# Attention weights transposed by transfers instead of on TensorE, in a two-layer graph kernel

## The chip, the cores and the metric

The kernel runs on one core of one Trainium2 chip. The core has five instruction queues that run on their own and meet at semaphores: TensorE (PE in the profile, its weight loads PEld), VectorE (DVE), ScalarE (ACT), GpSimd (POOL) and SyncE (SP), which here issues nearly all transfers. PE reads SBUF and writes PSUM, which the program uses as eight banks of 128 x 512 float32. The metric is device time in microseconds of one execution, the median of several.

## What is computed

There are 64 graphs of 256 nodes with 256 features, `x` (64, 256, 256), and an integer adjacency `adj` (64, 256, 256). Cut to what matters:

```python
# layer 0: three rounds of message passing with a GRU cell
A = (adj != 0)
h = x
for i in range(3):
    m = h @ weight[i]
    aggr = einsum('bst,bsd->btd', A, m)
    h = gru_cell(aggr, h, w_ih, w_hh, b_ih, b_hh)   # r, z: sigmoid; n: tanh; (1-z)*n + z*h
v = layernorm(x + h)
# layer 1: graph attention
Wh = v @ W
e = leaky_relu((Wh @ a1)[:, :, None] + (Wh @ a2)[:, None, :], 0.2)
attn = softmax(where(adj > 0, e, -9e15), axis=2)
out = layernorm(v + attn @ Wh)
```

All of it is float32. The gate matmuls are split into three parts (upper, lower, cross) whose sum comes close to float32.

## The kernel before

Graphs are worked on in **pairs**: 32 pairs p of two graphs (G = 2), each of C = 2 chunks of 128 nodes, so K = 4 chunks a pair. Each pair goes through three **blocks** (p, i), one for each round i of layer 0, and then through `attention`. Blocks are interleaved: one **turn** is the blocks (q, 0), (q-1, 1), (q-2, 2), and the attention of pair q-2 starts when its third block is done, beside the next turns.

**Order of the work.** Nothing is reordered after the program is written out; each engine takes its instructions in program order. The program makes this order with a small clock. `gates` writes the 72 matmuls of a block and calls `tick()` after every group of six (L469, L474): 12 ticks a block, 36 a turn. Everything else is a step put down for a tick with `at(t, step)` or `after(dt, step)` (L89, L93), and `tick` writes out all steps that are due; of steps of one tick, those put down first come first. So a tick fixes where an instruction stands in its queue and no time. After the last block the clock just jumps from step to step: this is the end of the run, with no gate matmuls beside it.

**A block's front.** `front` (L383), due from the start of the block ahead, prepares the operands: the hidden state's upper part on ACT (L419), its lower part on POOL (L423) and its cross part on DVE (L427), and the aggregation `aggregate` (L437) with its parts (L440 to L446). The tuples CLOSE, LOOSE and FIRST (L679 to L681) say at which ticks: the first six are turn, split, rest, aggregate, a_upper, a_rest, the last three h_upper, h_lower, h_cross.

**A block's gates.** `product` (L458) accumulates into two PSUM banks, pga and pgb; ACT empties the first (L471, L473) and DVE the second (L475). The gate chain behind goes through DVE, ACT (sigmoid and tanh, L484) and POOL (L492, L493, L498, L502), and ends with DVE's addition into the state hT (L505). `lags` are the ticks from the last product to tanh, blend and that addition.

**Transposes by transfer.** TensorE and a transfer can both transpose. The transfer takes 16-bit elements, so a float32 tile is seen as two 16-bit planes: a DMA transpose (`turn_half`, L295, or L345 for x) turns them, `gather` (L300, four transfers) brings the halves of each plane together, and two strided 16-bit copies, `put_together` (L278), interleave the planes to float32 again. Before the change x (from pair 5 on: `x_turned`, `x_joined`), the state between rounds (`h_turned`) and v (in `attention`) are turned so. In `put_together` ACT copies the upper plane; the lower goes to ACT for h (with `k`) and to DVE for x and v.

**Attention.** From tick t on (L544): the kept x is loaded again (L551) and h added to it (L553, vT), vT turned to v (L572 to L575), layer norm statistics (L578), `project` (L589), `spread` (L598, L600: ACT for k < 2, DVE for the others), `rows` (L608), `scores` (L612), the mask from the adjacency loaded a second time (L625), `masked` (L631), maximum (L633), exponentials `exps` (L636). Then `weights_T` transposes the weights on PE, four 128 x 128 pieces for each graph into a PSUM bank (L651), DVE copies the bank over the weights in SBUF (L669), `combine` multiplies by Wh (L659), `add` adds it to v (L665), and a second layer norm and the store follow (L676).

**Buffers** are tags of the pools, each with so many copies. Of `late`: "wh", "sc" and "vT" one, "v" two. Of `io`: "x" and "adj" one each. In "adj" stand, in turn, the adjacency, the second stage of x's and of h's (round 1) transposes, and the adjacency again. A tile waits until the last reader of its tag's former tenant is done. `room` gives the last two pairs' attention other buffers.

Of the kernel before, what the change touches and what calls it, by code (L numbers as in the profile page):

```python
# [9 lines left out]
F32 = mybir.dt.float32  # L10
# [9 lines left out]
P = 128  # L20
# [7 lines left out]
def kernel(  # L28
# [60 lines left out]
    def at(t, step):  # L89
        clock[1] += 1  # L90
        heappush(pending, (t, clock[1], step))
# [19 lines left out]
    def evacuate(dst, src):  # L111
        copies[0] += 1
        if copies[0] % 2:
            nc.scalar.copy(dst, src)
        else:
            nc.vector.tensor_copy(dst, src)

    def flat(t):
        return t.rearrange("p a b -> p (a b)")
# [155 lines left out]
            nc.tensor.transpose(pt[:, k * P:(k + 1) * P], src[:, k // C, k % C, d * P:(d + 1) * P], ident)  # L275
        after(1, lambda: evacuate(dst[:, d, :], pt))

    def put_together(dst, hi, lo, k=None):  # L278

        dst = dst.bitcast(U16).rearrange("p (n h) -> p h n", h=2)  # L280
        if k:
            dst = dst.rearrange("p h (k n) -> p h k n", k=k)
        nc.scalar.copy(dst[:, 1], hi)
        if k:
            nc.scalar.copy(dst[:, 0], lo)
        else:
            nc.vector.tensor_copy(dst[:, 0], lo)
# [17 lines left out]
    def h_turned(p, i, e):  # L305

        s = pairs[p]
        pool, tags, dt = ((late, ("wh", "sc"), (16, 19, 22)), (io, ("x", "adj"), (12, 22, 25)))[i]
        tmp = {}

        def first():
            tmp["a"] = first_of(pool.tile([P, G, C, D], F32, tag=tags[0], name=f"first_h{p}_{i}"))
            for d in range(C):
                turn_half(tmp["a"], s.hT, d)

        def second():
            tmp["b"] = second_of(pool.tile([P, G, C, D], F32, tag=tags[1], name=f"second_h{p}_{i}"))
            gather(tmp["b"], tmp["a"])

        def join(d):  # L320
            tmp[d] = work.tile([P, K, P], F32, tag="V", name=f"V{d}_{p}_{i}", bufs=1)
            put_together(tmp[d].rearrange("p k n -> p (k n)"),
                         *(tmp["b"][:, h, :, d * P:(d + 1) * P] for h in (1, 0)), k=K)

        def split(d):
            s.hi[d] = work.tile([P, K, P], F32R, tag=f"hi{d}", name=f"hi{d}_{p}_{i + 1}", bufs=1)
            nc.scalar.copy(s.hi[d], tmp[d])

        def rest(d):
# [28 lines left out]
    def x_joined(p):  # L358
        begin(p)
        s = pairs[p]  # L360
        for d in range(C):
            put_together(s.hT[:, d, :], s.halves[:, 1, d, :], s.halves[:, 0, d, :])

    def from_T(hT, d):
        pt = bank("pt")
# [178 lines left out]
    def attention(p, t):  # L544
# [47 lines left out]
        def spread(k):  # L592
            rs = s.rs[:, k:k + 1]
            for dst, src in ((s.s1[:, k:k + 1], pts[k][:, D:D + 1]),
                             (s.s2[:, k, :], pts[k][:, D + 1:D + 2].to_broadcast([P, P])),
                             (s.wh[:, k // C, k % C, :], pts[k][:, :D])):
                if k < 2:
                    nc.scalar.activation(dst, src, AF.Copy, scale=rs)  # L598
                else:
                    nc.vector.tensor_scalar(dst, src, rs, None, op0=ALU.mult)  # L600
        for k in range(K):
            at(t + 37 + k, lambda k=k: project(k))
            at(t + 38 + k, lambda k=k: spread(k))

        def rows():
            pts[0] = bank("s2")
# [16 lines left out]
        def mask():  # L623
            s.mask = work.tile([P, K, N], U8, tag="mask", name=f"mask_{p}", bufs=1)
            nc.vector.tensor_scalar(s.mask, loaded_adj.pop(p).rearrange("p g c n -> p (g c) n"), 0.0, None,  # L625
                                    op0=ALU.is_le)
        at(t + 38, adj_again)
        at(t + 43, mask)

        def masked():  # L630
            nc.vector.copy_predicated(flat(s.sc), flat(s.mask), neg.to_broadcast([P, K * N]))  # L631
# [4 lines left out]
            nc.scalar.activation(s.sc[:, k, :], s.sc[:, k, :], AF.Exp, bias=s.nm[:, k:k + 1],  # L636
                                 accum_out=s.sm[:, k:k + 1])
        for k in range(K):
            at(t + 47 + k // 2, lambda k=k: exps(k))

        def divide():

            nc.vector.tensor_mul(s.sm, s.sm, s.rs)
            nc.vector.reciprocal(s.sm, s.sm)
        at(t + 52, divide)

        def weights_T(g):
            pts[g] = bank("pt")
            for j in range(C):
                for c in range(C):  # L650
                    nc.tensor.transpose(pts[g][:, (j * C + c) * P:(j * C + c + 1) * P],  # L651
                                        s.sc[:, g * C + c, j * P:(j + 1) * P], ident)

        def combine(g):
            eT = s.sc[:, g * C:(g + 1) * C, :]
            pts[g] = bank("po")
            for c in range(C):
                for j in range(C):
                    nc.tensor.matmul(pts[g][:, c * D:(c + 1) * D], eT[:, j, c * P:(c + 1) * P], s.wh[:, g, j, :],  # L659
                                     start=(j == 0), stop=(j == C - 1))  # L660

        def add(g):
            for c in range(C):
                k = g * C + c
                nc.vector.scalar_tensor_tensor(s.v[:, g, c, :], pts[g][:, c * D:(c + 1) * D], s.sm[:, k:k + 1],  # L665
                                               s.v[:, g, c, :], op0=ALU.mult, op1=ALU.add)
        for g in range(G):
            at(t + 51 + g, lambda g=g: weights_T(g))
            at(t + 52 + g, lambda g=g: nc.vector.tensor_copy(flat(s.sc[:, g * C:(g + 1) * C, :]), pts[g]))  # L669
# [12 lines left out]


    blocks = []
# [43 lines left out]
    for n, (p, i) in enumerate(blocks):  # L728
        if n + 1 < len(blocks):
            np_, ni = blocks[n + 1]  # L730
            if ni == 0:
                if np_ < FROM:
                    after(1, lambda p=np_: begin(p))
                after(1, lambda p=np_: take_x(p))
                after(3, lambda p=np_: ones(p))
                nxt = np_ + 1
                if nxt < FROM:
                    after(7, lambda p=nxt: load_x(p))
                elif nxt < NP:
                    later = {}  # L740
                    after(25, lambda p=nxt, d=later: d.update(f=x_turned(p)))
                    after(29, lambda d=later: d["f"]())
                    after(32, lambda p=nxt: x_joined(p))
                    after(32, lambda p=nxt: load_x(p))
                after(5 if nxt < FROM else 34, lambda p=nxt: load_adj(p))
            front(np_, ni, clock[0], 
                  CLOSE if n and np_ == blocks[n - 1][0] or ni == 2 and np_ >= FROM else LOOSE if ni else FIRST)
        gates(p, i, (2, 3, 5) if n + 2 >= len(blocks) or blocks[n + 2][0] == p else (4, 5, 10))
        if i == L - 1:
            attention(p, clock[0])  # L750
        elif FROM <= p and p + i + 1 < NP:
            h_turned(p, i, clock[0])
# [32 lines left out]
```

## Time and profile before

| what | us |
|---|---|
| median of 3 runs | 2135.44 (2135.32 to 2135.72) |
| the profiled execution | 2135.01 |
| its span, first to last instruction | 2133.2 |
| PE busy in it | 2087.5 |
| DVE, ACT, POOL busy in it | 1788.7, 1609.8, 1605.2 |
| mean granted TensorE clock | 0.991 |

The span is 1.8 us shorter than the execution's own time; the rest lies around it. A row of a group reads: line, engine, operation, output<-inputs, shapes, count | busy time of all, mean ns of one | idle time of the engine just before them, and what ended it. Overlapping instructions count once in busy time. A row of a timeline is start, length, engine, line, operation, tiles and count; neighbours of one kind are merged.

### The profile page before, as it was taken

Reading aid. Unit: us, or ns where it says so; the run is one execution under the profiler, and the core shown is the slowest. Engines: PE = TensorE matmul, PEld = TensorE weight load, DVE = VectorE, ACT = ScalarE, POOL = GpSimd, SP = SyncE. Lnnn points to the kernel's source line nnn. Section 1 sums busy time; section 2 is a strip of 40 time slices with the busy share of each in tenths; the row PEclk is TensorE's granted clock in tenths of the full one; section 3 lists DMA queues with packets and bytes.
Section 4 is the critical chain, followed back from the end, with each engine's and each line's share of the span. In section 5 each row is a group of like instructions: output and inputs, shape, how many; then the busy total and the mean of one; then the engine's idle time right before and its main releaser. Section 6 shows DMA issues by size and latency. Waiting matters only on the chain.

```text
span 2133.2 us, 30903 instructions
## 1 busy us (share of the span) xinstructions
PE 2087.5 (98%) x10100; PEld 1748.8 (82%) x10100; DVE 1788.7 (84%) x2885; ACT 1609.8 (75%) x2938; POOL 1605.2 (75%) x1114
## 2 busy tenths in 40 slices
PE   8999999999999999999999999999999999999985
PEld 6788888888888888888888888888888888888864
DVE  5667788898889898888889888989888989888775
ACT  4566677778787777888777888787888787878664
POOL 6677687787788787788787787878777878778661
PEclk9999999999999999999999999999999999999997
DMA  4011324445545545445545544554544644543232
GB/s 128 30 40 40 67 73 119 99 99 129 115 103 129 120 107 129 109 100 128 129 109 119 110 111 116 129 120 108 129 102 110 135 119 99 131 111 85 50 75 74
DMA packets 416865, 220.68 MB, mean 103 GB/s; under 512 B 241792, under 2 KB 408448, under 8 KB 416704
## 3 DMA queue, kind: packets, MB, share of 16 engines
q1 hardware_dynamic: 414912, 216.86, 43.5%
q8 instruction: 80, 1.31, 0.3%
q10 hardware_dynamic: 1616, 1.57, 0.2%
q14 instruction: 81, 0.66, 0.1%
q0 software_dynamic: 176, 0.27, 0.1%
HBM read 69.74 MB, written 33.55 MB: 48 GB/s over the span
## 4 chain that ended last, share of the span: by engine, by line
PE 94%; DVE 2%; POOL 1%; ACT 1%; issue 1%; DMA 0%; POOLq 0%; ACTq 0%; SPq 0%; DVEq 0%
PE pga L466 48%; PE pgb L466 24%; PE pa L437 8%; PE po L659 5%; PE pwh L589 5%; PE pt L651 1%; PE s L608 1%; PE pt L367 1%; DMA rows_hH<-in_L_gnn_w_hh_dram 0%; PE pw L236 0%; POOL n L502 0%; DVE sc L631 0%; DVE cut L133 0%; POOL t L492 0%; DVE nm L633 0%
## 5 line engine op out<-in xcount | busy, mean ns | idle before, releaser
L492 POOL TENSOR_TENSOR t<-hT,n 128x512 f32<-128x512 f32 x192 | 253.1, 1318 | 391.1 <-ACT n L484 391.0
L466 PE MATMUL pga<-hH,whhH_whh 128*128 128x512 f32 x1152 | 378.2, 409 | 0.0
L466 PE MATMUL pgb<-hD,whhD_whh 128*128 128x512 f32 x1152 | 359.5, 393 | 1.2 <-DVE hD L136 1.2
L466 PE MATMUL pga<-hL,whhL_whh 128*128 128x512 f32 x1152 | 357.1, 391 | 0.0
L493 POOL TENSOR_TENSOR t<-t,z 128x512 f32<-128x512 f32 x192 | 291.3, 1517 | 15.1
L471 ACT ACTIVATE r<-pga 128x512 f32<-128x512 f32 x192 | 114.8, 598 | 242.4 <-PE pga L466 130.9
L502 POOL TENSOR_TENSOR n<-n,t 128x512 f32<-128x512 f32 x192 | 281.0, 1464 | 21.4 <-DVE t L475 11.1
L498 POOL TENSOR_TENSOR n<-n,r 128x512 f32<-128x512 f32 x192 | 288.4, 1502 | 4.5 <-DVE n L475 4.5
L475 DVE SCALAR_TENSOR_TENSOR r<-pgb,r 128x512 f32<-128x512 f32 x192 | 131.3, 684 | 166.4 <-ACT r L471 139.9
L133 POOL TENSOR_TENSOR hL<-hT,hH 128x1024 fp32r<-128x1024 f32 x96 | 255.7, 2664 | 13.3 <-ACT hH L130 13.2
L466 PEld LDWEIGHTS pgb<-hD,whhD_whh 128*128 128x128 f32 x1152 | 214.0, 188 | 55.2 <-issue 8.4
L466 PEld LDWEIGHTS pga<-hL,whhL_whh 128*128 128x128 f32 x1152 | 216.4, 188 | 47.9 <-POOL hL L133 0.4
L466 PEld LDWEIGHTS pga<-hH,whhH_whh 128*128 128x128 f32 x1152 | 206.3, 189 | 31.9
L437 PE MATMUL pa<-A,hi 128*128 128x256 f32 x768 | 200.0, 293 | 0.0
L437 PE MATMUL pa<-A,lo 128*128 128x256 f32 x768 | 192.0, 283 | 0.0
L136 DVE SCALAR_TENSOR_TENSOR hD<-hH,hT 128x1024 fp32r<-128x1024 f32 x96 | 186.4, 1942 | 0.0
L505 DVE TENSOR_TENSOR hT<-t,n 128x512 f32<-128x512 f32 x192 | 171.3, 893 | 5.6 <-POOL t L493 5.6
L484 ACT ACTIVATE r<-r,b_sum 128x512 f32<-128x512 f32 x192 | 140.4, 731 | 42.7 <-DVE r L475 42.0
L473 ACT ACTIVATE n<-pga,bh 128x512 f32<-128x512 f32 x192 | 133.5, 696 | 50.7 <-PE pga L466 46.4
L471 ACT ACTIVATE t<-pga 128x512 f32<-128x512 f32 x192 | 115.3, 601 | 57.3 <-DVE hT L505 38.2
L475 DVE SCALAR_TENSOR_TENSOR t<-pgb,t 128x512 f32<-128x512 f32 x192 | 131.0, 682 | 25.6 <-ACT t L471 22.5
L437 PEld LDWEIGHTS pa<-A,lo 128*128 128x128 f32 x768 | 146.3, 191 | 6.2 <-issue 0.2
(142 smaller groups left out, 5474.0 us busy)
## 6 DMA issues: line engine op xcount, KB each, us to landing
adj<-in_adj_dram SPq DMA_DIRECT2D x64, 512.0 KB, 4.2
second<-first SPq DMA_DIRECT2D x236, 128.0 KB, 3.2
second_h<-first_h SPq DMA_DIRECT2D x204, 128.0 KB, 3.4
x<-in_x_dram SPq DMA_DIRECT2D x32, 512.0 KB, 4.2
xT<-hT SPq DMA_DIRECT2D x32, 512.0 KB, 3.0
vT<-xT SPq DMA_DIRECT2D x32, 512.0 KB, 4.4
out_dram<-v SPq DMA_DIRECT2D x32, 512.0 KB, 3.2
first_h<-hT SPq DMA_TRANSPOSE x102, 3.5
```

The source lines that it names most:

```text
L133: eng.tensor_sub(dst, src, hi.bitcast(F32))
L136: nc.vector.scalar_tensor_tensor(dst, hi.bitcast(F32), 1.0 + U, src, op0=ALU.mult, op1=ALU.subtract)
L437: nc.tensor.matmul(pt[:, g * N:(g + 1) * N], h[:, g * C + c, :], s.A[:, g, c, :], start=(n == 0), stop=(n == len(todo) - 1))
L466: nc.tensor.matmul(pt, w[:, d, o * P:(o + 1) * P], m[:, d, :], start=n in (0, ends + 1), stop=n in (ends, len(todo) - 1))
L471: nc.scalar.activation(dst, a, AF.Copy, scale=1.0 + U)
L475: nc.vector.scalar_tensor_tensor(dst, b, -1.0 / U, dst, op0=ALU.mult, op1=ALU.add)
L484: nc.scalar.activation(dst, dst, func, bias=bias)
L492: nc.gpsimd.tensor_sub(t, h, n)
L493: nc.gpsimd.tensor_mul(t, t, z)
L498: after(2, lambda r=r, n=n: nc.gpsimd.tensor_mul(n, n, r))
L502: after(1, lambda n=n, t=t: nc.gpsimd.tensor_add(n, n, t))
L505: after(lags[2], lambda n=n, t=t, h=h: nc.vector.tensor_add(h, t, n))
```

## The change

- **Weights by transfer.** For pairs p < 30 (`by_dma = p < NP - 2`) `turn_weights` issues one DMA transpose for each graph from the weights `sc` into a new tile `eT`, which has the tag "v"; `gather_weights` brings the planes' halves back into `sc`'s place (four transfers each), and `join_weights` interleaves the planes into `eT` by two copies on ACT. `combine` reads `eT`, and `add` writes its result there instead of over v (`s.o`). Pairs 30 and 31 keep PE's transposes and DVE's copy.
- **Half-way results in v's place.** The transpose of vT goes into v's own tile instead of into "wh", and h's second stage of round 0 into "adj" instead of into "sc".
- **Copies of planes.** `put_together` is told the engines, upper plane first: h of round 0 ACT and DVE, h of round 1 DVE and ACT (both were ACT's); v ACT for both (the lower was DVE's); x as it was.
- **Timetable.** Ticks of most attention steps move, the lags of the gates become (2, 5, 9) for (4, 5, 10), and each round has its own tuple for the front.

The diff, cut to its core:

```diff
+    ENGINES = {"a": nc.scalar.copy, "v": nc.vector.tensor_copy, "g": nc.gpsimd.tensor_copy}
...
-    def put_together(dst, hi, lo, k=None):
...
 
...
-        nc.scalar.copy(dst[:, 1], hi)
-        if k:
-            nc.scalar.copy(dst[:, 0], lo)
-        else:
-            nc.vector.tensor_copy(dst[:, 0], lo)
+        for h, src in ((1, hi), (0, lo)):
+            ENGINES[engines[1 - h]](dst[:, h], src)
...
-        pool, tags, dt = ((late, ("wh", "sc"), (16, 19, 22)), (io, ("x", "adj"), (12, 22, 25)))[i]
+        pool, dt = ((late, (16, 19, 22)), (io, (12, 22, 25)))[i]
...
-            tmp["a"] = first_of(pool.tile([P, G, C, D], F32, tag=tags[0], name=f"first_h{p}_{i}"))
...
+            tmp["b"] = second_of(io.tile([P, G, C, D], F32, tag="adj", name=f"second_h{p}_{i}"))
             gather(tmp["b"], tmp["a"])
...
-                         *(tmp["b"][:, h, :, d * P:(d + 1) * P] for h in (1, 0)), k=K)
+                         *(tmp["b"][:, h, :, d * P:(d + 1) * P] for h in (1, 0)), "av" if i == 0 else "va", k=K)
...
-                at(e + dt[2] + 3 * d + n, lambda step=step, d=d: step(d))
+                at(e + dt[2] + (2, 4)[i] * d + n, lambda step=step, d=d: step(d))
...
-        at(t + 5, again)
-        at(t + 14, lambda: nc.vector.tensor_add(flat(s.vT), flat(s.vT), flat(s.hT)))
+        at(t + 7, again)
+        at(t + 13, lambda: nc.vector.tensor_add(flat(s.vT), flat(s.vT), flat(s.hT)))
...
 
             if d == 0:
-                s.first = first_of(room("wh", [P, G, C, D], p, "first"))
-            turn_half(s.first, s.vT, d)
+                s.v = room("v", [P, G, C, D], p)
+            turn_half(first_of(s.v), s.vT, d)
...
             s.halves = second_of(room("sc", [P, G, C, D], p, "second"))
-            gather(s.halves, s.first)
+            gather(s.halves, first_of(s.v))
...
         def join(g):
-            if g == 0:
-                s.v = room("v", [P, G, C, D], p)
...
-                         *(s.halves[:, h, ks].rearrange("p k d -> p (k d)") for h in (1, 0)))
+                         *(s.halves[:, h, ks].rearrange("p k d -> p (k d)") for h in (1, 0)), ("aa", "aa")[g])
         for d in range(C):
-            at(t + 20 + d, lambda d=d: turn(d))
-        at(t + 24, second)
+            at(t + 24 + d, lambda d=d: turn(d))
+        at(t + 29, second)
         for g in range(G):
-            at(t + 28 + g, lambda g=g: join(g))
+            at(t + 32 + g, lambda g=g: join(g))
...
-            s.rs, s.eps = layer_norm(s.v, f"a_{p}", (t + 31, t + 33))
-        at(t + 30, norm)
+            s.rs, s.eps = layer_norm(s.v, f"a_{p}", (t + 34, t + 36))
+        at(t + 34, norm)
...
-        at(t + 38, adj_again)
-        at(t + 43, mask)
+        at(t + 37, adj_again)
+        at(t + 41, mask)
...
-            at(t + 47 + k // 2, lambda k=k: exps(k))
+            at(t + 46 + k // 2, lambda k=k: exps(k))
...
-        at(t + 52, divide)
+        at(t + 51, divide)
...
+        def turn_weights(g):
+
+            if g == 0:
+                s.eT = late.tile([P, G, C, C, P], F32, tag="v", name=f"eT_{p}", bufs=2)
+            nc.sync.dma_start_transpose(s.eT[:, g].rearrange("p c j n -> p (c j n)").bitcast(U16)
+                                        .rearrange("p (q n) -> p q n", n=P),
+                                        s.sc[:, g * C:(g + 1) * C, :].rearrange("p c n -> p (c n)").bitcast(U16))
+
+        def planes(g):
+            return s.sc[:, g * C:(g + 1) * C, :].rearrange("p c n -> p (c n)").bitcast(U16).rearrange(
+                "p (h m n) -> p h m n", h=2, n=P)
+
+        def gather_weights(g):
+            gather(planes(g), s.eT[:, g].rearrange("p c j n -> p (c j n)").bitcast(U16).rearrange(
+                "p (m b n) -> p m b n", b=2, n=P))
+
+        def join_weights(g):
+            dst = s.eT[:, g].rearrange("p c j n -> p (c j n)").bitcast(U16).rearrange("p (n h) -> p h n", h=2)
+            for h in (1, 0):
+                ENGINES[("aa", "aa")[g][1 - h]](dst[:, h], planes(g)[:, h].rearrange("p m n -> p (m n)"))
+
         def combine(g):
-            eT = s.sc[:, g * C:(g + 1) * C, :]
             pts[g] = bank("po")
             for c in range(C):
                 for j in range(C):
-                    nc.tensor.matmul(pts[g][:, c * D:(c + 1) * D], eT[:, j, c * P:(c + 1) * P], s.wh[:, g, j, :],
+                    if by_dma:
+                        e = s.eT[:, g, c, j, :]
+                    else:
+                        e = s.sc[:, g * C + j, c * P:(c + 1) * P]
+                    nc.tensor.matmul(pts[g][:, c * D:(c + 1) * D], e, s.wh[:, g, j, :],
                                      start=(j == 0), stop=(j == C - 1))
...
         def add(g):
+
+            if by_dma:
+                s.o = s.eT.rearrange("p g c j n -> p g c (j n)")
+            else:
+                s.o = s.v
             for c in range(C):
                 k = g * C + c
-                nc.vector.scalar_tensor_tensor(s.v[:, g, c, :], pts[g][:, c * D:(c + 1) * D], s.sm[:, k:k + 1],
+                nc.vector.scalar_tensor_tensor(s.o[:, g, c, :], pts[g][:, c * D:(c + 1) * D], s.sm[:, k:k + 1],
                                                s.v[:, g, c, :], op0=ALU.mult, op1=ALU.add)
+        by_dma = p < NP - 2
         for g in range(G):
-            at(t + 51 + g, lambda g=g: weights_T(g))
-            at(t + 52 + g, lambda g=g: nc.vector.tensor_copy(flat(s.sc[:, g * C:(g + 1) * C, :]), pts[g]))
-            at(t + 54 + g, lambda g=g: combine(g))
-            at(t + 55 + g, lambda g=g: add(g))
+            if by_dma:
+                at(t + 50 + g, lambda g=g: turn_weights(g))
+                at(t + 52 + g, lambda g=g: gather_weights(g))
+                at(t + 56 + g, lambda g=g: join_weights(g))
+            else:
+                at(t + 51 + g, lambda g=g: weights_T(g))
+                at(t + 52 + g, lambda g=g: nc.vector.tensor_copy(flat(s.sc[:, g * C:(g + 1) * C, :]), pts[g]))
+            at(t + (58 if by_dma else 54) + g, lambda g=g: combine(g))
+            at(t + (58 if by_dma else 54) + 1 + g, lambda g=g: add(g))
...
-            nc.sync.dma_start(out[p * G:(p + 1) * G].rearrange("g (c p) d -> p g c d", p=P), s.v)
+            nc.sync.dma_start(out[p * G:(p + 1) * G].rearrange("g (c p) d -> p g c d", p=P), s.o)
...
-        at(t + 60, lambda: layer_norm(s.v, f"b_{p}", (t + 61, t + 64, t + 66, t + 70), s.eps, store))
+        at(t + 60, lambda: layer_norm(s.o, f"b_{p}", (t + 60 + 1, t + 64, t + 66, t + 71), s.eps, store))
...
     CLOSE = (5, 5, 5, 7, 8, 8), (6, 6, 7)
-    LOOSE = (2, 3, 4, 6, 7, 8), (5, 8, 10)
-    FIRST = (2, 1, 2, 6, 7, 8), (5, 8, 10)
+    EARLY = (2, 1, 2, 6, 7, 8), (5, 8, 10)
+    FIRST = (2, 1, 2, 7, 7, 8), (3, 10, 7)
+    SECOND = (2, 3, 4, 6, 7, 8), (3, 8, 10)
+    THIRD = (2, 3, 4, 7, 8, 9), (3, 6, 7)
...
-                after(3, lambda p=np_: ones(p))
+                after(2, lambda p=np_: ones(p))
...
-                    after(25, lambda p=nxt, d=later: d.update(f=x_turned(p)))
-                    after(29, lambda d=later: d["f"]())
-                    after(32, lambda p=nxt: x_joined(p))
-                    after(32, lambda p=nxt: load_x(p))
+                    after(26, lambda p=nxt, d=later: d.update(f=x_turned(p)))
+                    after(30, lambda d=later: d["f"]())
+                    after(33, lambda p=nxt: x_joined(p))
+                    after(33, lambda p=nxt: load_x(p))
                 after(5 if nxt < FROM else 34, lambda p=nxt: load_adj(p))
...
-                  CLOSE if n and np_ == blocks[n - 1][0] or ni == 2 and np_ >= FROM else LOOSE if ni else FIRST)
-        gates(p, i, (2, 3, 5) if n + 2 >= len(blocks) or blocks[n + 2][0] == p else (4, 5, 10))
+                  CLOSE if n and np_ == blocks[n - 1][0] else
+                  EARLY if np_ < FROM and not ni else (FIRST, SECOND, THIRD)[ni])
+        gates(p, i, (2, 3, 5) if n + 2 >= len(blocks) or blocks[n + 2][0] == p else (2, 5, 9))
```

More of the change, by code (lines that the diff above doesn't have):

```diff
@@ L276, in to_T, with put_together @@
         after(1, lambda: evacuate(dst[:, d, :], pt))
-    def put_together(dst, hi, lo, k=None):
+    def put_together(dst, hi, lo, engines, k=None):
         dst = dst.bitcast(U16).rearrange("p (n h) -> p h n", h=2)
@@ L307, in h_turned @@
         s = pairs[p]
-        pool, tags, dt = ((late, ("wh", "sc"), (16, 19, 22)), (io, ("x", "adj"), (12, 22, 25)))[i]
+        pool, dt = ((late, (16, 19, 22)), (io, (12, 22, 25)))[i]
         tmp = {}
         def first():
-            tmp["a"] = first_of(pool.tile([P, G, C, D], F32, tag=tags[0], name=f"first_h{p}_{i}"))
+            tmp["a"] = first_of(pool.tile([P, G, C, D], F32, tag=("wh", "x")[i], name=f"first_h{p}_{i}"))
             for d in range(C):
@@ L316, in second @@
         def second():
-            tmp["b"] = second_of(pool.tile([P, G, C, D], F32, tag=tags[1], name=f"second_h{p}_{i}"))
+            tmp["b"] = second_of(io.tile([P, G, C, D], F32, tag="adj", name=f"second_h{p}_{i}"))
             gather(tmp["b"], tmp["a"])
@@ L361, in x_joined @@
         for d in range(C):
-            put_together(s.hT[:, d, :], s.halves[:, 1, d, :], s.halves[:, 0, d, :])
+            put_together(s.hT[:, d, :], s.halves[:, 1, d, :], s.halves[:, 0, d, :], ("av", "av")[d])
     def from_T(hT, d):
@@ L596, in spread @@
                              (s.wh[:, k // C, k % C, :], pts[k][:, :D])):
-                if k < 2:
+                if k in (0, 1):
                     nc.scalar.activation(dst, src, AF.Copy, scale=rs)
@@ L602, in attention @@
             at(t + 37 + k, lambda k=k: project(k))
-            at(t + 38 + k, lambda k=k: spread(k))
+            at(t + 37 + 1 + k, lambda k=k: spread(k))
         def rows():
```

## The prediction

> **What bounds the kernel now.** I read the page first: busy shares, then the chain that ended last.
>
> ```profile
> span 2133.2 us, 30903 instructions
> PE 2087.5 (98%) x10100; PEld 1748.8 (82%) x10100; DVE 1788.7 (84%) x2885; ACT 1609.8 (75%) x2938; POOL 1605.2 (75%) x1114
> PE 94%; DVE 2%; POOL 1%; ACT 1%; issue 1%; DMA 0%; POOLq 0%; ACTq 0%; SPq 0%; DVEq 0%
> ```
>
> PE is on 94% of the chain. A busy PE may still be a slow one, so next come the totals of single stretches, one turn (63.46 us, below) in the middle and the end:
>
> ```profile
> 1000.00:1063.46 63.46, 63.46 (x310) 53.38 (x309) 55.89 (x90) 51.04 (x94) 49.91 (x35) 1.00 0.50 117
> 2067.00:2133.00 66.00, 34.88 (x134) 26.37 (x132) 41.29 (x104) 27.60 (x74) 12.40 (x16) 0.77 0.40 96
> ```
>
> Columns: length; busy of PE, PEld, DVE, ACT, POOL; granted clock; DMA share; GB/s. In mid-run PE has no gap at all: what it doesn't execute is saved, and a wait of another engine counts only once PE stands. The last gate matmul ends at 2067.4; the 66 us behind it are a chain of latencies through all engines, in which PE work is nearly free and latency is dear. So the change has two prices, one per stage.
>
> The length of a turn is read from the transpose of x, once a turn on SP's timeline (63.44 and 63.48 us apart):
>
> ```profile
> 1131.44 1.88 SPq L345 DMA_TRANSPOSE first<-in_x_dram  x1
> 1194.88 1.33 SPq L345 DMA_TRANSPOSE first<-in_x_dram  x1
> 1258.36 2.03 SPq L345 DMA_TRANSPOSE first<-in_x_dram  x1
> ```
>
> A turn has 36 ticks of 1.76 us.
>
> **PE's transposes.** The groups by shape, and PE's timeline where eight of them lie:
>
> ```profile
> L651 PE MATMUL pt<-ident,sc 128*128 128x128 f32 x256 | 41.9, 288 | 16.7 <-ACT sc L636 16.7
> ...
> L669 DVE COPY sc<-pt 128x512 f32<-128x512 f32 x64 | 42.9, 672 | 0.0
> ```
>
> ```profile
> 1010.86 0.63 PE L466 MATMUL pgb<-hD,whhD_whh 128*128 128x512 f32 x2
> 1011.32 0.60 PE L651 MATMUL pt<-ident,sc 128*128 128x128 f32 x4
> 1011.68 0.71 PE L466 MATMUL pga<-hH,whhH_whh 128*128 128x512 f32 x2
> 1012.23 0.62 PE L466 MATMUL pga<-hL,whhL_whh 128*128 128x512 f32 x2
> 1012.69 0.63 PE L466 MATMUL pga<-aH,wc1H_wc 128*128 128x512 f32 x2
> 1013.15 0.60 PE L651 MATMUL pt<-ident,sc 128*128 128x128 f32 x4
> 1013.51 0.72 PE L466 MATMUL pga<-aL,wc1L_wc 128*128 128x512 f32 x2
> 1014.06 0.62 PE L466 MATMUL pgb<-hD,whhD_whh 128*128 128x512 f32 x2
> ```
>
> Gate matmuls go at 0.456 us a pair (1012.23 to 1012.69). From 1010.86 to 1014.06 are five pairs, 2.28 us, but 3.20 passed: eight transposes cost 0.92 us, 0.115 each, for one attention. This isn't the 288 ns of a single one, which overlap. Here the Trainium skill would mislead: "TensorE: Matmul & The Clock Gate", Part 4, has about 275 ns for a PE transpose in a kernel. Durations here agree (288), yet 232 of them at 275 would be an estimated 64 us of saving; by start-to-start spacing it is 232 x 0.115 = 26.6. The spacing decides.
>
> Why 232: the 24 for pairs 29 to 31 all start after 2067.4 (at 2081.65, 2101.40, 2104.31, 2115.02), so pairs 0 to 28, 29 attentions, lie where PE is full. All 29 go to transfers: **-26.6 us**, a turn of 62.54. Pairs 30 and 31 keep PE; pair 29 is of the tail, below.
>
> **What takes their place,** per turn of 62.54 us, each beside PE's work:
>
> SP: two transposes and eight gathers. By tile, one first_h transpose takes SP 1.33 us (median), one second_h gather 0.62; landing 3.4 us for both. 2 x 1.33 + 8 x 0.62 = 7.6 us of issue on SP's 23.9 now (sum over the turn from 1194.88), so 31.5. They are due at ticks 14 to 17, behind the transpose of x and ahead of x's gather (18). That slot is idle now: SP's timeline has the transpose end at 1196.2 and the gather start at 1206.8, 10.6 us, plus one tick by which the gather's releaser moves back: 12.3. Needed: 3.4 (first landing) + 8 x 0.62 = 8.3. It fits with 4 us left; beyond that x's join, the next adjacency and the mask are late in turn.
>
> ACT: weights' planes, four copies at 0.77 us (L283), +3.1; v's low planes come from DVE, two, +1.5; four of the eight copies of h's planes leave, -3.1. Together +1.5 on 51.0: 52.6 of 62.54, 84%. The exponentials run ahead of the weights' joins by 10 ticks.
>
> DVE: L669 goes, -1.3; v's planes go, -1.4; four copies of h's planes come. Their price isn't in the trace, but the same copy is, twice:
>
> ```profile
> L287 DVE COPY v<-second x64: 444/468/1190, 205.0 to 2094.9; 128x512 uint16<-128x512 uint16 x64
> ...
> L287 DVE COPY hT<-second x54: 448/1554/1897, 258.8 to 1913.4; 128x512 uint16<-128x512 uint16 x54
> ```
>
> Bounds 0.45 and 1.9 us; the slow ones lie under POOL instructions in the timeline (at 1023.00 under hL's 3.4 us). The Trainium skill, "SBUF — State Buffer", says why and speaks against this change: VectorE and GpSimd share a port pair as an exclusive lock, the loser waits the other's whole instruction. With POOL busy 49.9 of 63.46 us, the rule would put nearly every copy at 1.9: 4 x 1.9 - 2.7 = +4.9, DVE at 60.8 of 62.54. By the means (692 and 1577 ns), between which I take the middle, 1.13: 4.5 - 2.7 = +1.8, 57.7 or 92%. I take the rows: some v copies met POOL and still cost 0.47. On the path: nothing, while DVE keeps up.
>
> The timetable: x, ones, mask and exponentials move by one tick, v's transfers by four or five, at no cost of work. The moved h_lower (10 for 8 in FIRST) keeps its place among POOL's instructions, between the additions of one gate and the next blend. Tanh two ticks earlier (lag 2 for 4) takes from POOL its largest wait, 391 us for ACT's n (12 a turn), but ACT now waits for POOL's addition: 0.6 to 1.4 us each where lag 2 already stands at the end (2045.51, 2072.15), six a turn, 4 to 8 us against ACT's 10 idle. Behind it on ACT stand evacuations of PSUM: PE has eight banks, and two fewer groups take them. From the end of each bank's last reader to the start of the eighth next group, the timeline leaves a median of 2.9 us for pga and 3.9 for pgb, so 1 to 2 us of lateness is absorbed. Likely cost 0; without that cover, up to a few us a turn. Single buffers get tighter: "adj" now holds h's first-layer planes too, five tenants a turn in a chain, and v's transpose (24) waits for the last addition of the pair before (24). Bounds: 0 (PE is full, so nothing here can gain) to +1.5 us a turn; I take 0.
>
> **The tail.** Here pair 29's weights go by transfer though PE is idle, and pair 30's and 31's work stands behind them in every queue. The chain now:
>
> ```profile
> 2081.00 1.83 ACT sc L636 x7
> ...
> 2084.12 3.02 PE po L659 x8
> ...
> 2093.15 0.48 ACT wh L598
> ...
> 2095.51 1.62 ACT sc L612 x4
> ...
> 2114.37 2.09 ACT sc L636 x8
> ```
>
> Exponentials of 29 end at 2083.0, pair 30's spread starts 2092.7, exponentials of 31 2114.4, the end 2133.2. The mask, now ahead of the last state addition, brings 29's exponentials to 2082.3 (two done at 2081.4). Then SP, in order: transpose 0 issued 2081.4, transpose 1 2083.0, gathers 0 from 2085.3 (landing), 2.5 us, gathers 1 from 2087.9, and only then pair 30's own gather, 2090.5 instead of 2077.2 (tick 53 for both, 29's pushed first); it lands about 2095.7. ACT copies in order: 29's planes 0, pair 30's 0 (2095.7), 29's 1, pair 30's 1, ends 2099.8. DVE statistics 2100.9, POOL's root 1.9 later: spread of 30 at 2102.8, **10 us late**. Pair 31's own transfers are behind too (landing 2103), but its joins now come after 30's scores, so 31's exponentials start near 2123: +8.7. Bounds: +2 (landings as short as the minimum, orders that loosen) to +14 (a slow landing more). I take **+8.7**.
>
> **Sum.** Profiled execution 2135.0 (span 2133.2): 2135.0 - 26.6 + 8.7 = 2117.1; the median of the runs is 0.4 above it, so **2117.5 us**.
>
> **Rivals.**
> 1. The tail hides it: pair 30's path finds slack, nothing lost, 2135.4 - 26.6 = 2109. For: POOL idles 15.5 us there. Against: SP's queue is strict. 0.12.
> 2. Part is given back: PE stands 0.3 us a turn over 29 turns for a bank or an operand (L484 behind POOL, or x late): 2117.5 + 8.7 = 2126. For: banks come free only some 3 us ahead. 0.20.
> 3. Slower: DVE becomes the bound, in the turns with h by transfer (26). Place: h's copies at ticks 13, 17, 34, 36, under POOL. At 1.58 each (the hT row's mean) DVE has 55.9 + 6.3 - 2.7 = 59.5 us of work, and its wait for ACT's r (139.9 us, 4.4 a turn) stays: 63.9, 1.4 over 62.54, x 26 = 36: 2154. It decides once turns grow by 17.9 / 29 = 0.62 us. Against: that wait shrinks when DVE is late. 0.13.
> 4. It doesn't do what it says: freed PE time is spent waiting for what a turn needs anyway, turn near 63.2, 2135. Against: no gap on PE in the mid-run stretch. 0.05.
>
> **Chances.** Main case 0.50, its own range 2112 to 2124 (tail +3 to +14). By a difference of 0.2% (4.3 us), about what can be told from no change: faster 0.82 (main, 1, 2), same 0.05, slower 0.13. Range: leaving out rival 3 and the far ends, 2105 to 2134.
>
> **What would show it.** Right: L651 with 16 instructions, L669 with 4; turns 62.5 us apart; PE still gapless to about 2008; in the tail, SP gathers of the weights ahead of pair 30's, and 29's weights to the end some 9 us longer, about 75 us from the last gate matmul. Wrong: gaps on PE before pga or pa with ACT or DVE named; turns over 63.1; h's copies on DVE at 1.6 us and more; x's gather late behind the weights' gathers.

## The result, and the profile after

The changed kernel takes **2111.6 us** (2109.8 to 2114.4) against 2135.4: a ratio of 0.989, interval 0.9873 to 0.9907. Forecast were 2117.5 us, range 2105 to 2134. The profiled execution took 2112.9 us, with a span of 2111.1, 22.1 less than before.

First the page: the span, busy times of the engines, and the engines' shares of the chain that ended last.

```profile
span 2111.1 us, 31355 instructions
PE 2053.3 (97%) x9860; PEld 1726.3 (82%) x9860; DVE 1769.4 (84%) x2863; ACT 1659.1 (79%) x3020; POOL 1611.8 (76%) x1114
PE 93%; DVE 2%; POOL 2%; DMA 1%; ACT 1%; SPq 1%; issue 0%; POOLq 0%; ACTq 0%; DVEq 0%
```

PE has 240 instructions fewer and still bounds the run; ACT has more to do, DVE hardly less, and SP's queue and the transfers hold 1% of the chain each, where the page before had 0%. The two stages, in the totals of stretches (length; busy of PE, PEld, DVE, ACT, POOL; clock; DMA share; GB/s):

```profile
1000.00:1062.50 62.50, 62.50 (x302) 52.82 (x302) 56.14 (x90) 52.28 (x96) 50.30 (x35) 1.00 0.62 134
2034.50:2111.10 76.60, 33.41 (x124) 25.02 (x123) 40.15 (x102) 34.91 (x87) 13.61 (x19) 0.72 0.37 89
```

PE is still full in mid-run. From the start of a (q, 0) block's first gate matmul to that of the next, a turn is now 62.37 us, 63.48 before. The last gate matmul starts at 2034.1, 32.9 us earlier than before (2067.0); what lies behind it has grown from 66.2 to 77.0 us. Both parts went the way that was forecast. The extra time at the end, on SP's and ACT's timeline (start, length, line, operation, tiles; idle time before and what ended it):

```profile
2049.98 2.61 SPq L655 DMA_TRANSPOSE eT<-sc  x2
2053.34 5.27 SPq L302 DMA_DIRECT2D sc<-eT  x8
2058.66 2.88 SPq L302 DMA_DIRECT2D second<-v  x4
2060.60 1.38 ACT L670 COPY eT<-sc 128x512 uint16<-128x512 uint16 x2 [9.67 <-DMA sc<-eT]
```

Pair 29's eight gathers (sc<-eT) come out ahead of pair 30's four (second<-v), and ACT stands 9.7 us for them. Pair 30's spread starts 36.9 us after the last gate matmul, 25.7 before.

Three copies of planes, in the groups by shape (count | busy, mean ns of one | idle before):

```profile
L286 DVE COPY V<-second_h 128x512 uint16<-128x512 uint16 x102 | 85.8, 841 | 0.9
L670 ACT COPY eT<-sc 128x512 uint16<-128x512 uint16 x120 | 84.3, 772 | 16.1 <-DMA sc<-eT 15.8
...
L286 DVE COPY hT<-second 128x512 uint16<-128x512 uint16 x54 | 33.3, 670 | 0.7 <-DMA second<-first 0.7
```

The four copies new on DVE take 0.84 us each, and those of x, one tick later than before, fell from 1.58 to 0.67: before, 24 of the 54 started under POOL's `hL` and took 1.9 us, now none does. So DVE stays at 56.1 us a turn.

### The profile page after: what moved, and what is told of

Read it like the earlier page. It is cut to its first block, busy times and chain, and to the rows that moved or that the text cites. A ratio compares the mean times of both kernels' runs of the same rounds, so it can differ in the third digit from the quotient of the medians.

```text
span 2111.1 us, 31355 instructions
## 1 busy us (share of the span) xinstructions
PE 2053.3 (97%) x9860; PEld 1726.3 (82%) x9860; DVE 1769.4 (84%) x2863; ACT 1659.1 (79%) x3020; POOL 1611.8 (76%) x1114
## 4 chain that ended last, share of the span: by engine, by line
PE 93%; DVE 2%; POOL 2%; DMA 1%; ACT 1%; SPq 1%; issue 0%; POOLq 0%; ACTq 0%; DVEq 0%
PE pga L465 48%; PE pgb L465 24%; PE pa L436 8%; PE po L680 5%; PE pwh L586 5%; PE s L605 1%; PE pt L366 1%; SPq L302 1%; DMA rows_hH<-in_L_gnn_w_hh_dram 0%; DMA v<-vT 0%; POOL t L491 0%; POOL n L501 0%; DMA second<-v 0%; POOL t L492 0%; PE pw L238 0%
## 5 line engine op out<-in xcount | busy, mean ns | idle before, releaser
L491 POOL TENSOR_TENSOR t<-hT,n 128x512 f32<-128x512 f32 x192 | 264.2, 1376 | 186.2 <-ACT n L483 186.0
L497 POOL TENSOR_TENSOR n<-n,r 128x512 f32<-128x512 f32 x192 | 316.1, 1646 | 73.6 <-ACT r L483 48.5
L465 PE MATMUL pga<-hH,whhH_whh 128*128 128x512 f32 x1152 | 370.6, 403 | 0.0
L492 POOL TENSOR_TENSOR t<-t,z 128x512 f32<-128x512 f32 x192 | 271.0, 1411 | 15.0
L135 POOL TENSOR_TENSOR hL<-hT,hH 128x1024 fp32r<-128x1024 f32 x96 | 258.3, 2691 | 10.6 <-ACT hH L132 10.5
L138 DVE SCALAR_TENSOR_TENSOR hD<-hH,hT 128x1024 fp32r<-128x1024 f32 x96 | 202.4, 2109 | 0.0
L483 ACT ACTIVATE n<-n,bi 128x512 f32<-128x512 f32 x192 | 138.9, 723 | 75.5 <-POOL n L501 75.4
L436 PE MATMUL pa<-A,hi 128*128 128x256 f32 x768 | 193.6, 285 | 0.2 <-DVE A L377 0.2
L504 DVE TENSOR_TENSOR hT<-t,n 128x512 f32<-128x512 f32 x192 | 187.6, 977 | 5.9 <-POOL t L492 5.9
L436 PE MATMUL pa<-A,lo 128*128 128x256 f32 x768 | 192.1, 283 | 0.0
L135 DVE TENSOR_TENSOR aL<-pa,aH 128x512 fp32r<-128x512 f32 x192 | 131.1, 683 | 63.8 <-ACT aH L132 63.7
L132 ACT ACTIVATE aH<-pa 128x512 fp32r<-128x512 f32 x192 | 115.9, 604 | 64.0 <-PE pa L436 64.0
L483 ACT ACTIVATE z<-z,b_sum 128x512 f32<-128x512 f32 x192 | 140.7, 733 | 18.9 <-DVE z L474 18.1
```

The lines of the kernel that those rows point to most:

```text
L135: eng.tensor_sub(dst, src, hi.bitcast(F32))
L138: nc.vector.scalar_tensor_tensor(dst, hi.bitcast(F32), 1.0 + U, src, op0=ALU.mult, op1=ALU.subtract)
L436: nc.tensor.matmul(pt[:, g * N:(g + 1) * N], h[:, g * C + c, :], s.A[:, g, c, :], start=(n == 0), stop=(n == len(todo) - 1))
L465: nc.tensor.matmul(pt, w[:, d, o * P:(o + 1) * P], m[:, d, :], start=n in (0, ends + 1), stop=n in (ends, len(todo) - 1))
L483: nc.scalar.activation(dst, dst, func, bias=bias)
L491: nc.gpsimd.tensor_sub(t, h, n)
```

## The experiments

Time is compared with runs of the kernel before on the same chip (2134 to 2135 us). "Turn" is the length of most turns from the eighth on (the first is the one with block (0, 0) alone), "end" the time from the last gate matmul's start to the end of the span. The time before the third turn varies from run to run (100.8 to 103.6 us). Where weights aren't turned at all, the attention output of pairs 0 to 29 is not the reference's.

### All weights on TensorE, in the new timetable

```diff
-        by_dma = p < NP - 2
+        by_dma = False
```

> The changed kernel with all pairs' weights on TensorE's transposes; timetable, lags and engines of the plane copies stay changed. Theory (the transposes are the gain): turns go from 62.37 to 63.3 us, 29 x 0.94 = 27 us are lost and the tail's 10.8 are won back: 2128, so 7 below the kernel before, from the timetable. Rival (the timetable is the gain): turns stay near 62.5, 2101 to 2105.

Measured 2129.1 us, ratio 0.9971 (0.9959 to 0.9982); turn 63.38, end 65.9: the theory. From the third turn to the last gate matmul it needs 1958.2 us, the changed kernel 1931.5, the kernel before 1963.8. So taking the 232 transposes off TensorE is worth **26.7 us** in this timetable, and the rest of the change, with the transposes left in, 5.6 us.

The 26.7 us don't come evenly. The first three turns with attention get 0.87 us each shorter, the later ones 1.0, and the last three together 0.33, though they hold two attentions. Two waits stand behind that. The first row is a wait of the kernel with all weights on TensorE, which the changed kernel doesn't have; the second, of the changed kernel, comes 1.3 us long in the last three turns, where TensorE stands for the state:

```profile
PEld po L680 <- ACT V L286: 6.0, 25, 0.2
PE pt L366 <- DVE hT L504: 1.3, 1, 1.3
```

### No turning of the weights, in the new timetable

```diff
             if by_dma:
-                at(t + 50 + g, lambda g=g: turn_weights(g))
-                at(t + 52 + g, lambda g=g: gather_weights(g))
-                at(t + 56 + g, lambda g=g: join_weights(g))
+                pass
```

with `combine` reading `sc` and the tile `eT` made in `add`.

> The changed kernel without any turning of the weights of pairs 0 to 29: no transfers, no joins, no transposes; the products take the weights as they are, so the attention output of these pairs is not the reference's. It shows what the transfers and joins cost where TensorE is full. Theory: nothing there, turns stay 62.37 us; only the tail is shorter by 10 to 14: 2098 to 2102. Rival (transfers cost TensorE hidden waits): turns shorter than 62.3, under 2095.

Measured 2102.0 us, turn 62.37, end 62.3: the theory. Transfers and joins cost TensorE nothing in mid-run; at the end they cost 14.7 us. Two turns of 63.85 stand out here, of which more below.

### No turning of the weights, in the old timetable

```diff
-            at(t + 51 + g, lambda g=g: weights_T(g))
-            at(t + 52 + g, lambda g=g: nc.vector.tensor_copy(flat(s.sc[:, g * C:(g + 1) * C, :]), pts[g]))
+            if p >= NP - 2:
+                at(t + 51 + g, lambda g=g: weights_T(g))
+                at(t + 52 + g, lambda g=g: nc.vector.tensor_copy(flat(s.sc[:, g * C:(g + 1) * C, :]), pts[g]))
```

> The kernel before without the transposes and the copy of the weights of pairs 0 to 29, which are used as they are, so that the attention output of these pairs is not the reference's. It prices the eight transposes in the old timetable. Theory: 29 x 0.92 to 0.94 = 27 us where TensorE is full and about 2 us in the tail: 2106. Rival (freed time is spent waiting in the old timetable for the cross part or a bank): turns over 62.9, 2115 or more.

Measured 2115.4 us, ratio 0.9907 (0.9892 to 0.9922): the theory's 2106 fell. Turns begin with 62.49 and settle at 62.87. The waits of PE's weight loads (who waits on whom: us in total, times, longest):

```profile
PEld s L608 <- DVE sc L600: 8.7, 25, 0.7
PEld pgb L466 <- issue: 8.4, 28, 0.3
```

The second row is in the profile of before too. The first had 0.3 us in all there: now TensorE's weight load reaches `rows` some 0.35 us a turn before DVE has spread the last chunk. From the third turn to the last gate matmul only 19.2 of the 26.7 us arrive. The same transposes are worth over a quarter less in the old timetable, because DVE's spread is not as early as TensorE has become: that wait, 8.7 us in all on the weight loads, is about what is missing.

### One tick of the old timetable

The wait marked "issue" lies at 1008.93 in the kernel before, just after the state's cross part hD ends on DVE (1006.51 + 2.31):

```profile
1006.51 2.31 DVE L136 SCALAR_TENSOR_TENSOR hD<-hH,hT 128x1024 fp32r<-128x1024 f32 x1
1008.93 0.30 PEld L466 LDWEIGHTS pgb<-hD,whhD_whh 128*128 128x128 f32 x2 [0.29 <-issue]
```

```diff
-    LOOSE = (2, 3, 4, 6, 7, 8), (5, 8, 10)
+    LOOSE = (2, 3, 4, 6, 7, 8), (5, 8, 8)
```

> The kernel before with one number changed: LOOSE has the state's cross part on VectorE at tick 8 instead of 10. Theory (28 waits of 0.29 us of the weight load of pgb<-hD, marked issue, are for this cross part and cost TensorE 0.13 us a turn): turns fall from 63.48 to 63.35 us, some 3.5 us in all: 2131. Rival (those waits are only the sequencer's): turns stay 63.48.

Measured **2175.5 us**, ratio 1.0192: neither theory nor rival. That wait is gone, and the first turns with attention (the fifth to the seventh) are 0.14 to 0.18 us shorter than in the kernel before. But from the ninth on turns are 65.19, with a new row:

```profile
PEld po L659 <- issue: 39.7, 25, 1.6
```

The timeline of DVE, ACT and, in the last row, PE shows what happened:

```profile
1012.77 3.36 DVE L136 SCALAR_TENSOR_TENSOR hD<-hH,hT 128x1024 fp32r<-128x1024 f32 x1
1016.05 0.68 DVE L475 SCALAR_TENSOR_TENSOR r<-pgb,r 128x512 f32<-128x512 f32 x1
1016.77 0.72 ACT L484 ACTIVATE r<-r,b_sum 128x512 f32<-128x512 f32 x1 [2.17 <-DVE r L475]
1017.40 0.71 ACT L484 ACTIVATE n<-n,bi 128x512 f32<-128x512 f32 x1
...
1018.60 1.28 ACT L636 ACT_TABLE_LOAD   x1
...
1029.20 1.97 PE L659 MATMUL po<-wh,sc 128*128 128x256 f32 x8 [1.22 <-DVE sc L669]
```

The cross part now runs ahead of the gate's r on DVE and takes 3.4 us there, beside `hL` on POOL (2.4 us from 1012.65); ACT waits 2.2 us for r, and the exponentials behind it come late. The transposed weights' copy on DVE is late in turn, and `combine` stands for it. Some 0.15 us a turn were won and 1.9 lost.

### Two ticks of the old timetable, without the turning

```diff
-    LOOSE = (2, 3, 4, 6, 7, 8), (5, 8, 10)
+    LOOSE = (2, 3, 4, 6, 7, 8), (5, 8, 8)
-        gates(p, i, (2, 3, 5) if n + 2 >= len(blocks) or blocks[n + 2][0] == p else (4, 5, 10))
+        gates(p, i, (2, 3, 5) if n + 2 >= len(blocks) or blocks[n + 2][0] == p else (4, 5, 9))
```

> The kernel before without any turning of the weights of pairs 0 to 29 (attention output of these pairs not the reference's), plus two numbers of the timetable: cross part of LOOSE at tick 8 instead of 10, the state's addition at lag 9 instead of 10. Without the two numbers turns were 62.87. Theory (there TensorE waits 0.35 us a turn for the last spread on VectorE, behind a state addition, and 0.13 for the cross part; these two numbers lift both): turns 62.37 to 62.45, about 2104. Rival (the wait comes from VectorE's load in that stretch, whatever the order): turns stay over 62.7.

Measured 2192.7 us, turns of 66.0: the theory fell. The kernel leaves the transposes out, so TensorE stands at other places than above:

```profile
PEld pgb L466 <- issue: 48.7, 23, 2.3
PEld pa L437 <- ACT n L484: 31.1, 23, 1.5
```

Which of the two numbers does this, and by what order, was not tried apart.

### The old lags

```diff
-        gates(p, i, (2, 3, 5) if n + 2 >= len(blocks) or blocks[n + 2][0] == p else (2, 5, 9))
+        gates(p, i, (2, 3, 5) if n + 2 >= len(blocks) or blocks[n + 2][0] == p else (4, 5, 10))
```

> The changed kernel with the gates' lags of the kernel before, (4, 5, 10) instead of (2, 5, 9). Theory (the earlier tanh and state addition take 0.1 to 0.4 us of waits a turn off TensorE once its transposes are gone): turns 62.5 to 62.8, 2115 to 2124. Rival (the lags matter to POOL's waits alone): turns stay 62.37, 2112.

Measured 2125.0 us, ratio 0.9953 (0.9933 to 0.9972), turn 62.64: the theory, with the time 1 us above its range. The lags are worth 13 us here by the medians, 12 from the third turn to the last gate matmul. The wait is DVE's addition of the gate sum:

```profile
PEld pga L465 <- DVE t L474: 10.5, 23, 1.0
```

### h's planes all on DVE, or all on ACT

```diff
-                         *(...), "av" if i == 0 else "va", k=K)
+                         *(...), "vv", k=K)
```

> The changed kernel with all eight copies of h's planes of a turn on VectorE (four now). Four more copies at the 0.84 us that the four take now: VectorE goes from 56.15 to about 59.5 of 62.37 us a turn. Theory (VectorE has this room): turns stay within 0.3 us of 62.37, within 8 us in all. Rival (VectorE is at its limit, the waits for ScalarE stay): turns of 63.5 or more, 2145 or more.

Measured 2176.4 us, ratio 1.0196, turn 64.74: the rival. The same line with "aa":

> The changed kernel with all eight copies of h's planes of a turn on ScalarE, as in the kernel before. ScalarE goes from 52.35 to 55.4 of 62.37 us a turn, VectorE from 56.15 to 52.8. Theory (the move to VectorE was needed to make room on ScalarE for the weights' joins): turns of 62.8 or more, 2122 or more. Rival (ScalarE had the room): turns stay 62.37, 2112.

Measured 2158.1 us, ratio 1.0115, turn 64.29, more than the theory had. A stretch of each, all on DVE first:

```profile
1000.00:1062.40 62.40, 60.55 (x292) 50.73 (x291) 59.03 (x90) 48.56 (x90) 46.97 (x32) 1.00 0.64 135
```

```profile
1000.00:1062.37 62.37, 60.71 (x290) 51.01 (x288) 51.85 (x82) 52.46 (x97) 47.59 (x34) 1.00 0.59 129
```

and what PE's weight loads wait for, in the same order:

```profile
PEld pa L436 <- DVE lo L135: 47.6, 25, 1.9
```

```profile
PEld pa L436 <- DVE lo L135: 49.5, 25, 2.1
```

With all of them on DVE that engine is busy 59.0 of 62.4 us, with all on ACT no engine but PE is over 53, so there it isn't load. TensorE stands for the same operand, h's lower part `lo`, either way. For each half of h, two copies of planes, then the upper part on ACT, then the lower part on DVE follow each other. With all on ACT, the half that TensorE stands for looks like this in nearly every turn (25 of 26 such lower parts start under `hL`; here ACT, POOL, DVE and PE):

```profile
1018.35 1.43 ACT L286 COPY V<-second_h 128x512 uint16<-128x512 uint16 x2
1020.36 2.38 POOL L135 TENSOR_TENSOR hL<-hT,hH 128x1024 fp32r<-128x1024 f32 x1
1020.87 2.43 DVE L135 TENSOR_TENSOR lo<-V,hi 128x512 fp32r<-128x512 f32 x1
1023.35 0.39 PE L436 MATMUL pa<-A,lo 128*128 128x256 f32 x1 [1.66 <-DVE lo L135]
```

The two copies take 1.43 us, one behind the other. In the changed kernel the same half has them side by side, 0.78 on ACT and 0.96 on DVE, 1.14 together. The larger part is the row of DVE: the lower part takes 2.43 us instead of 0.68, because it now starts 0.5 us behind POOL's `hL` and ends 0.6 behind it. In the changed kernel both start together, and the lower part comes first, as shown further down. With all on DVE three of the four lower parts of a turn take about 1.7 us each, under a POOL instruction. So the split matters as latency just ahead of the aggregation: it decides whether `lo` comes ahead of `hL`. No run moves `hL` away while the copies stay on one engine, so how much each part costs is read from the rows only, and with all on DVE its load may count as well.

### Pair 29 on TensorE

```diff
-        by_dma = p < NP - 2
+        by_dma = p < NP - 3
```

> The changed kernel, but pair 29 keeps TensorE's transposes (weights by transfer for p < 29). Theory (the tail pays for pair 29's gathers ahead of pair 30's on SP): the stretch with gate matmuls stays as in the changed kernel, last gate matmul near 2034, and the tail behind it falls from 76.6 us to about 66: some 2101 us. Rival (the tail is longer because of the later ticks of v's transpose and of both of v's copies on ACT): the tail stays over 74 us, 2109 or more.

Measured **2105.7 us**, ratio 0.9864 (0.9848 to 0.9881), and once more beside the next two:

> The kernel with pair 29 on TensorE's transposes once more, beside the two below, to compare them on one chip: 2101 to 2108, with single turns of 63.85 us among those of 62.37 where VectorE's lower part of h and POOL's lower part of the state start together and POOL comes first.

2105.8 us, ratio 0.9865 (0.985 to 0.988). No version with the reference's output has a lower median; the two runs below lie within its noise.

```profile
2035.40:2101.60 66.20, 34.23 (x134) 25.76 (x132) 41.38 (x104) 32.59 (x83) 13.88 (x20) 0.79 0.36 87
```

The end is 66.3 us, where it was 77.0: the theory. The whole growth came from turning pair 29's weights by transfer. The later ticks of v's transpose and both of its copies on ACT cost nothing in sum. The span fell by 9.5 us, the median by 6. The first profile has two turns of 63.85 us. Here is the timeline of DVE and POOL in one of them, and behind the dots in an ordinary turn:

```profile
1002.09 2.94 DVE L135 TENSOR_TENSOR lo<-V,hi 128x512 fp32r<-128x512 f32 x1
1002.09 2.39 POOL L135 TENSOR_TENSOR hL<-hT,hH 128x1024 fp32r<-128x1024 f32 x1
...
1065.94 2.95 POOL L135 TENSOR_TENSOR hL<-hT,hH 128x1024 fp32r<-128x1024 f32 x1
1065.94 0.68 DVE L135 TENSOR_TENSOR lo<-V,hi 128x512 fp32r<-128x512 f32 x1
```

Both start at the same moment in both turns. In the first, DVE takes 2.94 us instead of 0.68, so POOL must have come first; in the second, POOL takes 0.56 longer. TensorE waits 1.2 us for the late lower part (PE, pa L436 at 1005.08), and the turn is 1.48 longer. The meeting is no accident: in this kernel, in the changed one and in the one without turning, 25 times in a run the two start within 0.01 us of each other. DVE lost two of the 25 here, two in the second profile of this kernel, two without turning and none in the changed kernel's.

### The two starts apart, and the last pairs earlier

Both runs are on top of pair 29 on TensorE, the second on top of the first too.

```diff
-    THIRD = (2, 3, 4, 7, 8, 9), (3, 6, 7)
+    THIRD = (2, 3, 4, 7, 8, 9), (3, 8, 7)
```

> As the one above, with THIRD's lower part of the state on POOL at tick 8 instead of 6, which puts it behind the gate's addition, so that it no longer starts together with VectorE's lower part of h. Theory (the turns of 63.85 us are lost races[...], 2.26 us for VectorE of which 1.48 reach TensorE): no turn over 62.5 us from the sixth on, 1 to 4 us faster than the one above and a narrower spread. Rival (they come from late transfers): such turns remain, no difference. A move of one step on a full engine can also bring a new wait, as it did in the kernel before: then turns over 62.6 throughout.

Measured 2107.4 us (2106.4 to 2109.2), ratio 0.9879 (0.9864 to 0.9893). Here and in the next run the two start at least 1.7 us apart, no lower part takes over 0.9 us, and the turns of 63.85 are gone. But most turns are 62.53, and two of 63.4 remain, at places where the run beside it has 62.86 and 63.17. The new wait:

```profile
PEld pwh L586 <- ACT r L470: 8.7, 24, 1.1
```

So the collision is the cause of the turns of 63.85, and moving it away costs as much as it saves. What makes the other two turns long stays open.

```diff
-            at(t + 24 + d, lambda d=d: turn(d))
-        at(t + 29, second)
+            at(t + (20 if p >= NP - 2 else 24) + d, lambda d=d: turn(d))
+        at(t + (24 if p >= NP - 2 else 29), second)
...
-            at(t + 32 + g, lambda g=g: join(g))
+            at(t + (28 if p >= NP - 2 else 32) + g, lambda g=g: join(g))
```

with statistics and root moved alike and the joins "av" for these pairs.

> As the one above, with v of the last two pairs turned at the ticks of the kernel before (20, 24, 28, statistics 31, root 33) and joined by ScalarE and VectorE together. Theory (the chain at the end now runs through v's transpose and gather of pair 30, some 7.5 us of transfers, because these ticks put them behind the exponentials of pair 29): the tail falls from 66 us to 60 to 64. Rival (another chain of the same length stands behind it): the tail stays 65 or more.

Measured 2106.8 us, end 67.2, against 66.9 in the run above: the rival. The transfers of v were on the chain in the first profile with pair 29 on TensorE (7.5 us). In the second profile of that same kernel the chain of the end has none, and the end is 67.3: a chain of the same length without them was there from the start.

## Why the prediction was right or wrong

**The sum.** Forecast -26.6 + 8.7 = -17.9; spans -22.1 = -26.7 (transposes) - 5.6 (timetable) + 10.8 (end) - 0.6 (start). The total is near because two misses have opposite signs: 5.6 us for a term taken as 0, and 2.1 more at the end. The median, 2111.6, lies just below the main case's own range of 2112 to 2124.

**The price of a transpose** was right in mechanism: it is the start-to-start spacing that counts. 26.6 us were forecast and 26.7 measured, between two kernels that differ in mid-run only in how the weights are turned. That these agree to 0.1 us is luck: a turn gave 0.87 us at first and 1.0 later, for 0.92 forecast, and the last three turns gave 0.33, for 1.84. By durations it would have been 64.

**"The timetable: I take 0"** is the term that failed. Its reason, that PE is full and nothing can gain, rested on the busy time of the stretch, in which ends of matmuls are modelled and short gaps vanish. Turns of 63.38 for 63.48 show 0.1 us in it, 2.8 us over the run; as much again comes in the last three turns. A row that I passed over ("pgb <- issue", 28 times 0.3 us) pointed to the first. With the transposes gone the timetable weighs more: between the two kernels without any turning it makes 62.37 of 62.87 us a turn, and from the third turn on 10.5 us, or 13.4 without the new one's two long turns. The lags alone, which I took for POOL's relief, are 12 to 13 us of the changed kernel. Where the gain of an edit lies in time freed on a full engine, that time is only won if the others are as early.

**The tail** was right in mechanism and order of queues; the size is 10.8 for 8.7. Pair 30's spread came 11.2 us later, 10 forecast. Pair 29 alone makes it, as the run with it on TensorE shows.

**SP's slot** was sized wrongly, which cost nothing. I had 4 us to spare ahead of x's gather; the weights' transposes wait for the exponentials, and the weights' gathers end as x's gather starts:

```profile
1180.00 1.26 SPq L655 DMA_TRANSPOSE eT<-sc  x1
1181.43 1.97 SPq L344 DMA_TRANSPOSE first<-in_x_dram  x1
1183.45 1.30 SPq L655 DMA_TRANSPOSE eT<-sc  x1
1184.91 5.30 SPq L302 DMA_DIRECT2D sc<-eT  x8
1190.32 2.55 SPq L354 DMA_DIRECT2D second<-first  x4
```

Turns without these transfers are equally long, so no cover is used up.

**DVE's copies** were sized at 1.13 us and took 0.84, against the upper bound of 1.9; DVE 57.7 forecast, 56.1 measured, since x's copies no longer start under POOL's `hL`. ACT's 52.6 was 52.3.

**Rival 3** did not come in the changed kernel, but it was one more group of copies away. It named 63.9 us a turn for 59.5 us of work on DVE; four copies more made 64.74, in which DVE is busy 61.3. Its reason was too narrow, since all on ACT is nearly as bad with DVE at 53.8 of 64.29.

**Rival 2** happens in another form, as single turns that DVE's start has lost to POOL's. The changed kernel's runs spread over 4.6 us; such turns (1.5 us each) and the start (up to 2.8 us) could make that, but its one profile has none, the longer turn in it is 62.71, and so this isn't shown. **Rivals 1 and 4** fell with the end and the turns.

## What to carry to other kernels

Price work taken off a full engine by the spacing of starts around it, and then ask whether every other engine's order lets that engine come earlier: here the same 26.7 us gave 19.2 without a new timetable. Where a stage is full and another is a chain of latencies, give each its own form of the same step; one pair more on TensorE at the end gave 6 us more. A tick moved alone can cost ten times what it wins (1.9 us a turn for 0.15, with DVE and ACT busy for over 80% of a turn), so look at what it is put ahead of. And look for instructions of two engines that start together: here a lower part that started 0.5 us behind the other engine's instruction took 2.4 us instead of 0.7, and TensorE stood 1.7 us for it.

## What the runs showed of the hardware

Of two instructions of DVE and POOL that start within 0.01 us of each other, one is late by nearly the whole of the other: DVE's took 2.94 against 0.68 us, beside 2.39 us of POOL. The Trainium skill, "SBUF — State Buffer", section "SBUF: two separate sides", has this lock for DVE instructions with two SBUF inputs against GpSimd; these lines agree. What I hadn't expected is that the winner changes from turn to turn of one program: DVE lost none to two of 25 in the profiles above, and a turn of 63.85 instead of 62.37 us came of it. The spread from run to run isn't explained by that alone: the kernel with pair 29 on TensorE took 2100.9 to 2106.3 us, but the last kernel above, where the two start at least 1.7 us apart, took 2106.2 to 2112.1.
